# Loading, normalising and turning each x tile in three successive attention passes instead of one

## The chip, the cores and the metric

The kernel runs on one NeuronCore of a Trainium2 chip. The metric is the device time of one execution in microseconds (us), taken as the median of several runs. The engines are named as the profile names them: PE is TensorE (matmuls; PEld its weight loads), DVE is VectorE, ACT is ScalarE, POOL is GpSimd, SP is SyncE, which issues most of the DMAs. All matmuls write to PSUM banks.

## The reference

A batch of 32 sequences of 100 tokens of width 512 passes through a layer norm, a causal cross attention with 16 heads of width 32, and a mixture-of-experts feed-forward. Only the first 100 context rows can be seen through the causal mask. What matters here is the first part:

```python
q = (layernorm(x) @ WQ.T); k = ctx @ WK.T; v = ctx @ WV.T      # 16 heads of 32
scores = einsum(q, k) / sqrt(32), causal; attn = softmax(scores)
y = einsum(attn, v) @ Wfc.T + bfc
x = x + y
# then: layernorm, gate, 16 experts with top-k tokens, a shared expert, and the sum
```

## The kernel before

The 3200 tokens are cut into 8 blocks of 400 tokens (4 sequences), and the 512 columns into 4 chunks of 128 (4 heads). One pass u of the attention loop, u = 0 to 31, stands for block sb = u // 4 and chunk c = u % 4. Everything in the loop is written out by hand under a manual schedule: the order of the program text is the order in which each engine gets its instructions, and every engine works through its own list in order. Matrix products that need full precision are made of three matmuls on a rounded high part and a low remainder of each operand (`mm3`, whose matmul is L55 in the profile); `split` makes the two parts, a cast on ACT (L100) and a subtraction on DVE (L101).

A pass of the loop is a software pipeline over three blocks of work, on PE in this order:

- `scores` of pass u-1 (L236), whose maxima DVE then takes (L247);
- the Q projection of pass u, into a bank of the pool `ps_kv`, copied out by ACT (L226);
- turns of the probabilities of pass u-2 for sequences 0 and 1 (`p_turn`, L277), into banks of the pool `ps_ms`, copied out by ACT (`p_keep`, L282);
- a K projection of a context block needed later, into `ps_kv`, copied out by ACT (L200) and stored;
- turns of the probabilities for sequences 2 and 3;
- a V projection, likewise in `ps_kv` (ACT copy L183). Context blocks have 3 tiles of 128 rows and 4 passes, so in every fourth pass, c = 0, there is no V projection;
- the turn of one x tile (`x_turn`, L167) into a bank of `ps_ms`, which `split` then casts and subtracts (L100, L101) into xnh and xnl, the operands of the Q projection of the next block;
- `values` of pass u-2 (L292), into a bank of `ps_ms`, copied out by ACT at the next pass (`y_keep`, L299).

The pools `ps_kv` and `ps_ms` have two banks each, used in turn; the single `scores` tile takes four.

The softmax of pass u-1 in pass u has two halves. Each is: maxima on DVE (L247), a subtraction on POOL (`sm_sub`, L256), exp on ACT (`sm_exp`, L260), a sum and a reciprocal on DVE (`sm_sum`, L265, L266), and a product on POOL (`sm_mul`, L271).

The x work for a tile of 100 tokens, tile (sb+1, c) in pass u, is: `x_load` one pass earlier (SP, L145, from a pool of five buffers), `x_stats` (DVE L152 and L153, then 1/sigma on POOL, L154 and L155), `x_norm` (DVE L161), and `x_turn`. In the text of the pass x_stats stands between the first two p_keep and the second exp, x_norm ahead of the second sum, x_turn after the V projection. POOL also makes the low parts of the context tiles (`ctx_split`, L135). In pass 13 `load_consts` loads the gate weights gr, which ACT (L568) and DVE (L569) then split. In passes 29 to 31 the first part of the feed-forward is woven in; after that the feed-forward runs, which takes the rest of the time.

Of the kernel before, what the change touches and what calls it, by code (L numbers as in the profile page):

```python
# [7 lines left out]
F32 = mybir.dt.float32  # L8
FR = mybir.dt.float32r
# [6 lines left out]
B, S, D, H, DK = 32, 100, 512, 16, 32  # L16
T = B * S
NE, CAP, FF = 16, 12, 1024
NC4 = D // 128
NFC = FF // 128  # L20
NSB = 8
SB = T // NSB
# [25 lines left out]
def mm3(nc, out, terms, first=True, last=True, by_term=False):  # L48

    seq = [(t, p) for p in ((0, 0), (0, 1), (1, 0)) for t in terms]  # L50
    if by_term:
        seq = [(t, p) for t in terms for p in ((0, 0), (0, 1), (1, 0))]
    n = len(seq)
    for i, (t, (a, b)) in enumerate(seq):
        r = nc.tensor.matmul(out, t[0][a], t[1][b],  # L55
                             start=(first and i == 0), stop=(last and i == n - 1))
    return r.ins


def attention(tc, K, F):  # L60
    nc = tc.nc
    with ExitStack() as ctx, ExitStack() as kvctx:
        def pool(name, bufs, stack=ctx, **kw):
            return stack.enter_context(tc.tile_pool(name=name, bufs=bufs, **kw))
# [19 lines left out]
        xnp = [pool("a_xn0", 1, kvctx, side="right"), xn1]  # L84
        scctx = ctx.enter_context(ExitStack())
        ps_kv = pool("a_kv", BUF["pj"], space=PSUM)
        ps_sc = pool("a_sc", BUF["sc"], scctx, space=PSUM, side="right")
        ps_ms = pool("a_ms", BUF["tr"], space=PSUM)
# [10 lines left out]
        def split(hi, lo, src, eng=None):  # L99
            nc.scalar.copy(hi, src)  # L100
            (eng or nc.vector).tensor_tensor(lo, src, f32(hi), ALU.subtract)  # L101

        def load_w(w, dk):
            r = raw.tile([128, D], F32, name="raw")
            nc.sync.dma_start(r, K.wA[w, :, dk, :])
            return r
# [14 lines left out]
        cur = {}  # L121

        def ctx_load(j, d):
            t0, n = KSTART[j] * 128, KVB[j] * 128
            cr = crp.tile([128, KMAX], F32, name="cr")
            nc.sync.dma_start(cr[:, 0:n], K.ctxT[d, :, t0:t0 + n])
            cur["cr", j, d] = cr
# [9 lines left out]
            cur.setdefault(("cl", j), []).append(l)  # L137

        def x_load(sb, b):
            if b == 0:  # L140
                cur["xh", sb] = xnp[sb % 2].tile([128, NC4, SB], FR, name="xnh")
                cur["xl", sb] = xnp[sb % 2].tile([128, NC4, SB], FR, name="xnl")
            xt = xp.tile([S, D], F32, name="xt")
            r0 = (sb * 4 + b) * S
            nc.sync.dma_start(xt, K.x[r0:r0 + S, :])  # L145
            cur["x", sb, b] = xt

        def x_stats(sb, b):
            st = stp.tile([S, 6], F32, name="bst")
            mv = stp.tile([S, 2], F32, name="mv")  # L150
            rs = stp.tile([S, 1], F32, name="rs")
            nc.vector.bn_stats(st, cur["x", sb, b])  # L152
            nc.vector.bn_aggr(mv, st)  # L153
            nc.gpsimd.tensor_scalar(rs, mv[:, 1:2], EPS, None, ALU.add)  # L154
            nc.gpsimd.tensor_tensor(rs, rs, K.nhalf[0:S, 0:1], ALU.pow)  # L155
            cur["mv", sb, b] = mv, rs

        def x_norm(sb, b):
            xt = cur["x", sb, b]
            mv, rs = cur["mv", sb, b]  # L160
            nc.vector.tensor_scalar(xt, xt, mv[:, 0:1], rs, ALU.subtract, ALU.mult)  # L161

        def x_turn(sb, b):
            xt = cur["x", sb, b]
            tp = ps_ms.tile([128, NC4, 128], F32, name="ms")
            for dk in range(NC4):
                nc.tensor.transpose(tp[:, dk, 0:S], xt[:, dk * 128:(dk + 1) * 128],  # L167
                                    K.ident[0:S, 0:S])
            cs = slice(b * S, (b + 1) * S)
            split(cur["xh", sb][:, :, cs], cur["xl", sb][:, :, cs], tp[:, :, 0:S])  # L170

        def vproj(j, i):
            ps = ps_kv.tile([128, D], F32, name="kv")
            cs = slice(i * 128, (i + 1) * 128)
            ch, cl = cur["ch", j], cur["cl", j]
            mm3(nc, ps, [((ch[d][:, cs], cl[d][:, cs]),
                          (WH[1][:, d, :], WL[1][:, d, :])) for d in range(NC4)],
                by_term=(j == 0))
            return ps

        def vkeep(j, i, ps):
            v = vtp.tile([128, D], F32, name="vt")
            nc.scalar.copy(v, ps)  # L183
            t0 = (KSTART[j] + i) * 128
            nc.sync.dma_start(K.vD[t0:t0 + 128, :], v)
# [17 lines left out]
        def kload(u):  # L203
            sb, c = divmod(u, NC4)
            kt = ktp.tile([128, SB], F32, name="kt")
            nc.sync.dma_start(kt, K.kD[:, c, sb * SB:(sb + 1) * SB])
            cur["k", u] = kt
# [61 lines left out]
        def sm_mul(u, hb):  # L269
            pv, sm = cur["p", u, hb][1], cur["sm", u, hb]  # L270
            nc.gpsimd.tensor_tensor(pv, pv, sm[:, :, None].to_broadcast([S, 8, S]), ALU.mult)  # L271
# [31 lines left out]
        NU = nsb * NC4  # L303
        blocks = range(2, len(KVB))

        def prologue():
            nc.gpsimd.dma_start(mask, K.mask)
            wk = [load_wc(0, 0)]
            for d in range(NC4):
                ctx_load(0, d)  # L310
            wk += [load_wc(0, c) for c in range(1, NC4)]
            wv = [load_w(1, 0), load_w(1, 1)]
            split_wc(0, 0, wk[0])
            for d in range(NC4):
                ctx_split(0, d, nc.vector)
            wv.append(load_w(1, 2))
            for b in range(2):
                x_load(0, b)
            p0 = kproj(0, 0)
            split_wc(0, 1, wk[1])  # L320
            wv.append(load_w(1, 3))
            kkeep(0, 0, p0)
            p0 = kproj(0, 1)
            split_wc(0, 2, wk[2])
            split_wc(0, 3, wk[3])
            for b in range(2, 4):
                x_load(0, b)
            for d in range(NC4):
                ctx_load(1, d)
            wq = [load_wc(2, 0), load_wc(2, 1)]  # L330
            kkeep(0, 1, p0)
            p0 = kproj(0, 2)
            split_w(1, 0, wv[0])
            split_w(1, 1, wv[1])
            kkeep(0, 2, p0)
            p0 = kproj(0, 3)
            split_w(1, 2, wv[2])
            x_stats(0, 0)
            split_w(1, 3, wv[3])
            wq += [load_wc(2, 2), load_wc(2, 3)]  # L340
            kkeep(0, 3, p0)
            p0 = vproj(0, 0)
            x_norm(0, 0)
            x_stats(0, 1)
            x_stats(0, 2)
            x_norm(0, 1)
            x_stats(0, 3)
            for d in range(NC4):
                ctx_split(1, d, nc.vector)
            x_norm(0, 2)  # L350
            x_norm(0, 3)
            vkeep(0, 0, p0)
            p0 = vproj(0, 1)
            split_wc(2, 0, wq[0])
            for d in range(NC4):
                ctx_load(2, d)
            x_load(1, 0)
            vkeep(0, 1, p0)
            for c in range(NC4):
                kkeep(1, c, kproj(1, c))  # L360
                if c == 0:
                    for b in range(4):
                        x_turn(0, b)
                if c:
                    split_wc(2, c, wq[c], nc.gpsimd)
                    ctx_split(2, c - 1)
                else:
                    kload(0)
            ctx_load(3, 0)
            vkeep(1, 0, vproj(1, 0))  # L370

        with tc.manual_schedule():
            prologue()
            for u in range(NU):
                sb, c = divmod(u, NC4)
# [5 lines left out]
                kv = mine and j in blocks  # L381
                vv = kv and ck < KVB[j]
# [2 lines left out]
                jl, dl = divmod(u + NC4 + 2 - KS, NC4)  # L385
                jl += 2
                xs = mine and sb + 1 < nsb
                end = u - (NU - 3)
                if mine:
                    if u > 0:  # L390
                        kload(u)
                    if jl in blocks and (jl, dl) != (3, 0):
                        ctx_load(jl, dl)
                    sn, bn = divmod(u + 5, NC4)
                    if sn < nsb:
                        x_load(sn, bn)
                if FC_AT <= u < FC_AT + NC4:
# [36 lines left out]
                if back is not None:  # L434
# [1 line left out]
                    p_turn(back, 1)  # L436
                    p_keep(back, 0)
                    p_keep(back, 1)
                if xs:
                    x_stats(sb + 1, c)  # L440
                if end == 0:
                    pr.split_y(1)
                if end == 2:
# [16 lines left out]
                if back is not None:  # L460
# [1 line left out]
                    p_turn(back, 3)  # L462
                    p_keep(back, 2)
                    p_keep(back, 3)
                if xs:
                    x_norm(sb + 1, c)
                if a is not None:
                    sm_sum(a, 1)
                    sm_mul(a, 1)
                if end == 0:  # L470
                    pr.split_y(2)
                if end == 1:
# [9 lines left out]
                if vv:  # L482
                    vkeep(j, ck, vproj(j, ck))
                if xs:
                    x_turn(sb + 1, c)
                if end == 0:
                    pr.fc(0)
                if end == 1:
# [563 lines left out]
```

## Time and profile before

| what | us |
|---|---|
| median of 3 runs | 1749.06 (1748.99 to 1749.1) |
| the profiled execution, own time | 1750.64 |
| its span, first to last instruction | 1748.8 |
| attention loop, scores of pass 0 to the last values | about 40 to 394 |
| PE busy over the span | 1698.7 |
| mean granted clock of PE, as a share of full speed | 0.987 |

A row of a timeline gives the start in us, the length, the engine, the line, the operation, what it writes and reads, and in brackets how long the engine was idle before it and what ended that. A run of equal instructions is drawn together (x4). A row of a stretch table gives the stretch, its length, the busy time of PE, PEld, DVE, ACT and POOL, the granted clock, and the DMA share and rate. The chain of waits gives start, length and what was at work.

### The profile page before, as it was taken

The page shows a single profiled execution, that of the slowest core. Times are in us where ns is not written, and L with a number is a line of the kernel's source. Part 1 is how long each engine was busy: PE and PEld are TensorE (multiplying, and loading weights), DVE is VectorE, ACT ScalarE, POOL GpSimd, SP SyncE. Part 2 cuts the span into 40 slices and gives each one's busy share as a digit, 9 for nine tenths or more (in the row PEclk, how much of TensorE's full clock was granted, in tenths as well). Part 3 has the DMA queues.
Part 4 walks back from the last instruction along what each step waited for, and adds up shares of the span by engine and source line. Part 5 has one row for each costly group of instructions (what it writes and reads, how often), then busy time and mean ns, then how long its engine had stood idle before and what let it go on. Part 6 is the DMA issues. An engine that isn't in the chain of part 4 may idle for free.

```text
span 1748.8 us, 27994 instructions
## 1 busy us (share of the span) xinstructions
PE 1698.7 (97%) x11072; PEld 1559.6 (89%) x11072; DVE 885.7 (51%) x2118; ACT 681.2 (39%) x1086; POOL 445.0 (25%) x399
## 2 busy tenths in 40 slices
PE   7999999989999999999999999999999999999996
PEld 6888888878888999999889999999999999999996
DVE  4877777775333333333454444444444444444431
ACT  4555555543112111211234444444444444444431
POOL 3777777661111011101020111110111111011111
PEclk9999999989999999999999999999999999999998
DMA  7444443534111101102154555554555554555531
GB/s 211 136 137 155 131 131 118 164 109 134 70 63 59 55 31 67 61 19 73 46 185 142 163 141 153 158 158 148 148 159 147 163 153 143 156 162 137 137 88 18
DMA packets 82995, 211.13 MB, mean 121 GB/s; under 512 B 9489, under 2 KB 35842, under 8 KB 82864
## 3 DMA queue, kind: packets, MB, share of 16 engines
q1 hardware_dynamic: 71792, 183.87, 32.2%
q0 software_dynamic: 10784, 25.21, 7.9%
q8 instruction: 87, 1.43, 0.3%
q14 instruction: 44, 0.36, 0.1%
q10 hardware_dynamic: 288, 0.27, 0.0%
HBM read 163.71 MB, written 45.60 MB: 120 GB/s over the span
## 4 chain that ended last, share of the span: by engine, by line
PE 91%; DVE 3%; DMA 2%; POOL 2%; ACT 1%; issue 1%; SPq 0%; POOLq 0%; ACTq 0%; DVEq 0%
PE gu L55 46%; PE dn L55 23%; PE kv L55 10%; PE m L55 3%; PE ms L277 2%; PE sc L236 2%; PE ms L292 1%; POOL p L256 1%; DMA big<-yD 1%; PE m L779 1%; DVE p L247 1%; PE ms L167 1%; DVE xt L161 1%; DMA kD<-kk 1%; PE m L894 1%
## 5 line engine op out<-in xcount | busy, mean ns | idle before, releaser
L55 PE MATMUL gu<-xh,whl 128*128 128x384 f32 (+1 forms) x3200 | 645.0, 333 | 1.3 <-ACT g L654 1.3
L55 PEld LDWEIGHTS gu<-xh,whl 128*128 128x128 f32 x3200 | 559.0, 188 | 18.8 <-ACT g L654 1.5
L55 PE MATMUL dn<-whl,hh 128*128 128x512 f32 x1168 | 372.4, 400 | 0.0
L627 DVE TENSOR_TENSOR whl<-wraw,whl 128x1536 fp32r<-128x1536 f32 (+1 forms) x138 | 242.1, 1755 | 241.9 <-ACT whl L626 241.8
L55 PE MATMUL gu<-xl,whl 128*128 128x384 f32 (+1 forms) x1600 | 338.1, 333 | 0.0
L55 PEld LDWEIGHTS gu<-xl,whl 128*128 128x128 f32 x1600 | 280.8, 188 | 0.0
L655 DVE TENSOR_TENSOR g<-g,gu 128x384 f32<-128x384 f32 (+1 forms) x200 | 108.7, 544 | 319.1 <-PE gu L55 316.8
L658 ACT CAST hh<-g 128x384 fp32r<-128x384 f32 (+1 forms) x200 | 100.9, 505 | 431.8 <-DVE g L655 431.8
L55 PEld LDWEIGHTS dn<-whl,hh 128*128 128x128 f32 x1168 | 213.3, 189 | 37.3
L626 ACT CAST whl<-wraw 128x1536 fp32r<-128x1536 f32 (+1 forms) x138 | 201.4, 1460 | 105.3 <-PE dn L55 103.4
L55 PE MATMUL dn<-whl,hl 128*128 128x512 f32 x584 | 230.9, 395 | 0.0
L654 ACT ACTIVATE g<-gu 128x384 f32<-128x384 f32 (+1 forms) x200 | 96.7, 484 | 312.5 <-PE gu L55 312.4
L793 POOL DMA_INDIRECT out_dram<-x,isl x48 | 77.5, 1615 | 365.5 <-ACT x L792 355.8
L659 DVE TENSOR_TENSOR hl<-g,hh 128x384 fp32r<-128x384 f32 (+1 forms) x200 | 111.8, 559 | 114.2 <-ACT hh L658 114.2
L768 POOL DMA_INDIRECT big<-xnD,isl x48 | 48.7, 1015 | 422.5 <-PE m L779 351.8
L55 PEld LDWEIGHTS dn<-whl,hl 128*128 128x128 f32 x584 | 109.8, 188 | 25.9
L271 POOL TENSOR_TENSOR p<-p,sm 100x800 f32<-100x800 f32 x64 | 101.2, 1583 | 51.0 <-DVE sm L266 36.6
L256 POOL TENSOR_TENSOR p<-p,mx 100x800 f32<-100x800 f32 x64 | 96.5, 1528 | 49.7 <-DVE mx L247 49.7
L837 POOL TENSOR_TENSOR x<-x,bfc 128x512 f32<-128x512 f32 x24 | 44.4, 1875 | 248.4 <-DMA x<-x 248.4
L247 DVE CUSTOM_DVE_ANT_0 p<-sc,mask 100x100 f32<-100x100 f32 x512 | 95.6, 257 | 16.6 <-PE sc L236 16.6
L265 DVE TENSOR_REDUCE sm<-p 100x8 f32<-100x800 f32 x64 | 62.7, 980 | 14.1 <-ACT p L260 14.1
L260 ACT ACTIVATE p<-p 100x800 f32<-100x800 f32 x64 | 56.2, 879 | 17.3 <-POOL p L256 17.3
(138 smaller groups left out, 1650.7 us busy)
## 6 DMA issues: line engine op xcount, KB each, us to landing
wraw<-wE SPq DMA_DIRECT2D x136, 768.0 KB, 4.5
xt<-x SPq DMA_DIRECT2D x32, 200.0 KB
vD<-vt SPq DMA_DIRECT2D x25, 256.0 KB, 2.1
kt<-kD SPq DMA_DIRECT2D x32, 200.0 KB, 4.9
v<-vD SPq DMA_DIRECT2D x8, 800.0 KB
x<-x SPq DMA_DIRECT2D x25, 256.0 KB, 5.1
xnD<-xn SPq DMA_DIRECT2D x25, 256.0 KB, 2.0
out_dram<-x SPq DMA_DIRECT2D x25, 256.0 KB, 2.2
```

The lines of the kernel that those rows point to most:

```text
L55: r = nc.tensor.matmul(out, t[0][a], t[1][b], start=(first and i == 0), stop=(last and i == n - 1))
L247: nc.vector.tensor_tensor_reduce(out=p[:, bb, h, :], in0=sc[:, h, cs], in1=mask, scale=ISCALE, scalar=NEG, op0=ALU.add, op1=ALU.max, accum ...
L256: nc.gpsimd.tensor_tensor(pv, pv, mx[:, :, None].to_broadcast([S, 8, S]), ALU.subtract)
L265: nc.vector.tensor_reduce(sm, pv, AX.X, ALU.add)
L271: nc.gpsimd.tensor_tensor(pv, pv, sm[:, :, None].to_broadcast([S, 8, S]), ALU.mult)
L626: nc.scalar.copy(h[:, cs], r[:, cs])
L627: nc.vector.tensor_tensor(l[:, cs], r[:, cs], f32(h[:, cs]), ALU.subtract)
L654: nc.scalar.activation(g[:, 0:t], pg[:, 0:t], AF.Gelu)
L655: nc.vector.tensor_tensor(g[:, 0:t], g[:, 0:t], pu[:, 0:t], ALU.mult)
L658: nc.scalar.copy(hh[:, 0:t], g[:, 0:t])
L659: nc.vector.tensor_tensor(hl[:, 0:t], g[:, 0:t], f32(hh[:, 0:t]), ALU.subtract)
L793: ins = nc.gpsimd.indirect_dma_start(out=self.K.out, out_offset=bass.IndirectOffsetOnAxis(ap=r.isl[:, i:i + 1], axis=0), in_=o, in_offset= ...
```

## The change

The three steps on an x tile are spread over three passes. The tile that pass u turns is now loaded in pass u-2 and normalised in pass u-1. In a pass, `x_stats` and `x_norm` work on the tile of the following pass; x_norm stands after the second sum and product of the softmax instead of ahead of them. The prologue loads two tiles of block 1 instead of one, and does the statistics and the normalisation of the first of them. The pair xnh, xnl is taken from its pool in the first turn of a block, no longer in its first load. In passes without a V projection the turn goes into a bank of `ps_kv`; otherwise it uses `ps_ms` as before. The lines of the functions move by three: x_turn's matmul is L170 in the kernel after, x_norm L158.

```diff
         def x_load(sb, b):
-            if b == 0:
-                cur["xh", sb] = xnp[sb % 2].tile([128, NC4, SB], FR, name="xnh")
-                cur["xl", sb] = xnp[sb % 2].tile([128, NC4, SB], FR, name="xnl")
             xt = xp.tile([S, D], F32, name="xt")
...
-        def x_turn(sb, b):
+        def x_turn(sb, b, own=True):
+            if b == 0:
+                cur["xh", sb] = xnp[sb % 2].tile([128, NC4, SB], FR, name="xnh")
+                cur["xl", sb] = xnp[sb % 2].tile([128, NC4, SB], FR, name="xnl")
             xt = cur["x", sb, b]
-            tp = ps_ms.tile([128, NC4, 128], F32, name="ms")
+            if own:
+                tp = ps_ms.tile([128, NC4, 128], F32, name="ms")
+            else:
+                tp = ps_kv.tile([128, D], F32, name="kv").rearrange("p (c t) -> p c t", c=NC4)
...
+            x_load(1, 1)
             ctx_load(3, 0)
+            x_stats(1, 0)
             vkeep(1, 0, vproj(1, 0))
+            x_norm(1, 0)
...
+                xn = divmod(u + 5, NC4) if u + 5 < NU else None
...
-                    sn, bn = divmod(u + 5, NC4)
+                    sn, bn = divmod(u + 6, NC4)
                     if sn < nsb:
                         x_load(sn, bn)
...
-                if xs:
-                    x_stats(sb + 1, c)
+                if xn:
+                    x_stats(*xn)
...
-                if xs:
-                    x_norm(sb + 1, c)
                 if a is not None:
                     sm_sum(a, 1)
                     sm_mul(a, 1)
+                if xn:
+                    x_norm(*xn)
...
                 if xs:
-                    x_turn(sb + 1, c)
+                    x_turn(sb + 1, c, vv)
```

## The prediction

> **What bounds the kernel now.** I read the page first, then TensorE's (PE's) waits over the attention stage, then the timeline of one pass, then the chain of waits through it. Of the page, section 1 and the clock row of section 2:
>
> ```profile
> PE 1698.7 (97%) x11072; PEld 1559.6 (89%) x11072; DVE 885.7 (51%) x2118; ACT 681.2 (39%) x1086; POOL 445.0 (25%) x399
> ```
>
> PE bounds the whole, so only its idle time and its clock can be won. PE's waits from 100 to 385 us begin with
>
> ```profile
> PE ms L167 <- DVE xt L161: 8.3, 5, 1.7
> ```
>
> that is, five times the turn of an x tile (L167) waits up to 1.7 us for its normalisation on VectorE (L161). Over the span it is 10.4 us in seven waits: 0.45 in pass u=1, and 1.64 to 1.67 in each of u = 4, 8, 12, 16, 20, 24. These six are the passes with c=0, which have no V projection. PE's timeline in u=24 (start, length, instruction, idle time before):
>
> ```profile
> 294.97 0.85 PE L277 MATMUL ms<-ident,p 100*100 100x100 f32 x8
> 297.48 0.53 PE L167 MATMUL ms<-ident,xt 100*128 100x100 f32 x4 [1.67 <-DVE xt L161]
> 298.77 0.96 PE L236 MATMUL sc<-kt,q 32*100 32x100 f32 x32
> ```
>
> The pass began with its scores at 288.98, so it took 9.79 us. Pass u=28 has no V projection and no x work at all, a control inside the kernel:
>
> ```profile
> 337.02 0.85 PE L277 MATMUL ms<-ident,p 100*100 100x100 f32 x8
> 338.51 0.89 PE L292 MATMUL ms<-pt,v 100*32 100x100 f32 x32 [0.64 <-ACT pt L282]
> 339.34 0.96 PE L236 MATMUL sc<-kt,q 32*100 32x100 f32 x32
> ```
>
> From scores at 331.00 it takes 8.34 us: with x gone, the copy of turned probabilities on ScalarE (ACT, L282) ends last. A pass with V takes 10.74, and there the V matmuls (some 2.8 us) hide the x work. The chain of waits in u=24 shows why x is late:
>
> ```profile
> 293.18 1.53 POOL p L256
> ...
> 294.99 0.58 POOL rs L155
> 295.59 1.76 DVE xt L161
> ...
> 297.48 0.53 PE ms L167 x4
> ```
>
> The tile's 1/sigma stands on GpSimd (POOL) behind both subtractions of the softmax, then the normalisation takes 1.76 us. The clock is a second cost. In stretches of 3.4 us (PE's busy time is the third number, the granted clock the third from the end):
>
> ```profile
> 252.00:255.40 3.40, 1.74 (x44) 1.29 (x46) 3.19 (x4) 2.22 (x7) 1.84 (x3) 1.00 0.53 154
> 255.40:258.80 3.40, 3.40 (x39) 3.20 (x40) 2.56 (x26) 0.49 (x1) 2.82 (x3) 0.57 0.43 147
> 122.40:125.80 3.40, 2.29 (x69) 1.96 (x70) 2.63 (x4) 1.85 (x5) 1.84 (x2) 1.00 0.78 220
> ```
>
> The stall of u=20 is followed by 3.4 us at about half clock; that of u=8, shared by two stretches, isn't. After u = 4, 12, 16, 20 the clock falls: starts of slow stretches, 81.5, 167.0, 211.3, 255.4, lie multiples of 3.41 apart. The passes from scores after u=4, 16, 20 take 12.26, 12.01 and 12.23 against 10.74; with 0.24 more for the values matmuls after u=16, about 1.5 us each.
>
> [...] the normalisation takes 0.50 us at the shortest, and 1.75 beside a POOL product.
>
> **The change, part by part.** Order and counts of matmuls are the same; the turn only writes another bank in passes without V. No engine gains or loses an instruction.
>
> (1) Turn in u=4..24. Its tile is now normalised a pass earlier, so the wait on L161 goes. Next late is what u=28 shows: the values wait for the copies. The turn (about 0.44 us of issue) fits into that 0.64. A pass falls from 9.79 to 8.34: 1.45 each. In u = 4, 8, 16, 20, 24: 5 x 1.45 = **7.25 us**. The V-less bank (kv) is free: q was copied out at 292.86, 2.8 before the turn. The kv bank is needed again by the K projection of the next pass, at about 300.6, and the split of the turn should end near 298.2. With kv used, values take the bank of the third probability turn, not the fourth, as in u=28.
>
> (2) u=12 wins nothing. Its successor waits for a load:
>
> ```profile
> 166.73 3.92 DMA gr<-gwT
> ```
>
> ACT sits in front of gr from 166.6 to 170.73, and VectorE (DVE) until 171.0, with softmax behind both. That load is issued after the K copy of u=12, which doesn't move, so the second half of pass 13 still starts at 175.69. PE comes 1.45 us earlier, without the slow stretch, and waits about 2.5 us for a bank that y's copy frees (171.4) and 1.6 before 175.69. This can slow the clock after it: 0 to 1.5, I take **-0.75**.
>
> (3) Clock after u = 4, 16, 20: with 0.2 us of idle time left in those passes, 3 x 1.5 = **4.5 us**. Bounds: 0 (as many slow stretches elsewhere) and 4.5.
>
> (4) DVE's new order: maxima, statistics, sum 0, sum 1, normalise, split of the turn (L101). In u=24 exp 1 on ACT ends at 295.68, so sum 1 runs 295.72 to 296.7, its reciprocal to 296.9[...] The end of the attention shows the same meeting:
>
> ```profile
> 357.01 1.29 POOL L837 TENSOR_TENSOR x<-x,bfc 128x512 f32<-128x512 f32 x1
> 358.26 1.71 POOL L271 TENSOR_TENSOR p<-p,sm 100x800 f32<-100x800 f32 x1
> ```
> ```profile
> 357.65 0.93 DVE L867 TENSOR_SCALAR xn<-x,mv,rs 128x512 f32<-128x512 f32 x1
> ```
>
> DVE waits for the first POOL instruction, goes through at its end (358.58), and the second takes 1.71 instead of 1.52. So here: normalised by about 297.35, product 1 ends 0.25 late at 298.85, the context split on POOL at 299.85, before the next subtraction (300.0). ACT casts the turn at 297.1 to 297.6, L101 ends at 298.2. The next scores start at 297.32, their first maximum can start at 298.35. Nothing late: **0**. If DVE loses, see rival B. In passes with V the turn comes 2.8 us later, which covers both orders.
>
> (5) Start. SP issues one x load (0.32 us) sooner, ahead of a context load used a pass later. It lands perhaps at 40.4 (5.1 us from issue to use at 25.40), so statistics, 1/sigma and normalisation of tile 1 stand ahead of tile 0's split on DVE (41.54 before, about 43 now), with pass 0's maxima behind. POOL's context split, 38.76 before, ends by about 43.4; its reader on PE comes at 44.68. Set against the wait in u=1: from +0.45 to -1.0, I take **0**. Later SP, with five x buffers for three tiles in flight, waits for nothing new.
>
> (6) Taking xnh and xnl at the turn adds no instruction; their last reader, a q projection, is a pass earlier: 0. The last pass's statistics (u=27) fall away against the added ones of the start: 0.
>
> Sum: 7.25 - 0.75 + 4.5 = 11.0 us. The profiled execution took 1750.64 (span 1748.8 and 1.84 around it) and would take 1739.6. The median of the runs, 1749.06, lies 1.58 lower: **1738.1**. All behind the attention is PE-bound or timed from it, and keeps the shift; the long waits at 366 to 384, four slow stretches, may meet other windows: +-1.5.
>
> **Rivals.** A difference of 0.2% is 3.5 us, about what a measurement can tell from no change.
> - A, as summed, 1735.5 to 1740.5: chance 0.70. With slow stretches returning elsewhere, 1742.6: 0.08.
> - B, [...] Normalisation ends near 298.85, L101 at 299.45, and the maxima start 1.1 late. Passes have some 0.1 slack there (copy ends 294.85, next turn 294.97), so the third probability turn of the next pass stalls 1.0. Gain 5 x 0.45 + 4.5 - 0.75 = 6.0: 1743.1. [...] against it, the rows above. 0.13.
> - C, the change doesn't free the turn: L161 was only the last of two close releasers, and something as late takes its place. Gain under 1: about 1748. Pass 28 speaks against. 0.05.
> - D, slower: [...] Normalised at 299.85, L101 to 300.45, maxima 2.1 late, a stall of 2.0 in the next pass: 5 x -0.55 = -2.75, slow clock as before, u=13 -0.75, and perhaps one more slow stretch: about 1754. It decides from 1.55 us of lateness. Against it, again the rows of (4). 0.04.
>
> A and B with their bounds give 1735.5 to 1744.5. Faster 0.90, within 0.2% 0.06, slower 0.04.
>
> **What would show it.** Right: no wait of L170's turn on L158; V-less passes near 8.3 us; normalisation near 0.5 us with product 1 near 1.75; no slow stretches after u = 4, 16, 20; a longer PE idle before 175 in pass 13. Wrong: 1.75 us for the normalisation and waits of probability turns on ACT's copies in passes 5, 9, 17 (B, D); another releaser at the turn (C).

## The result, and the profile after

The kernel after took 1738.3 us (median of 4 runs, 1737.56 to 1739.08), the kernel before 1749.08 beside it: a ratio of 0.9938, 95% interval 0.9926 to 0.9950. The profiled execution after took 1738.44, with a span of 1736.6. Timed again in a later batch (e10, below), the ratio was 0.9937, 0.9923 to 0.9950.

Section 1 of the page after has the same counts of instructions, and PE is busy for 6.4 us less: the stretches at half clock (granted 0.50 or 0.51 in the four that follow the turns of u = 4, 12, 16 and 20 before) are fewer (mean granted clock 0.992, against 0.987 before).

```profile
PE 1692.3 (97%) x11072; PEld 1554.9 (90%) x11072; DVE 858.2 (49%) x2118; ACT 679.3 (39%) x1086; POOL 447.5 (26%) x399
```

PE's waits from 100 to 375 us after; a row names the waiting line, what it waited for, total, times and longest:

```profile
PE ms L280 <- ACT pt L285: 3.7, 3, 2.6
PE ms L892 <- ACT pt L285: 3.5, 2, 3.2
PE ms L280 <- ACT y L302: 2.8, 1, 2.8
PE ms L295 <- ACT pt L285: 2.3, 6, 0.6
```

The turn of x (now L170) waits for its normalisation (now L158) nowhere. The last row is what is next late in V-less passes (c = 0, those without a V projection): the values matmuls stand behind ACT's copies of the turned probabilities. The third row is new, in pass 13. The first two rows lie at the end of the attention, from 335 us on, where the kernel before has such waits too. PE's timeline of u=24 after:

```profile
285.95 0.85 PE L280 MATMUL ms<-ident,p 100*100 100x100 f32 x8
286.64 0.51 PE L170 MATMUL kv<-ident,xt 100*128 100x100 f32 x4
287.47 0.89 PE L295 MATMUL ms<-pt,v 100*32 100x100 f32 x32 [0.33 <-ACT pt L285]
288.30 0.96 PE L239 MATMUL sc<-kt,q 32*100 32x100 f32 x32
```

The turn follows the probability turns without a wait, into a kv bank. From scores at 279.97 to scores at 288.30 the pass takes 8.33 us, the length of the control pass 28. VectorE and GpSimd in the same pass:

```profile
286.69 0.98 DVE L268 TENSOR_REDUCE sm<-p 100x8 f32<-100x800 f32 x1 [0.32 <-ACT p L263]
287.84 0.49 DVE L158 TENSOR_SCALAR xt<-xt,mv,rs 100x512 f32<-100x512 f32 x1
288.65 0.57 DVE L101 TENSOR_TENSOR xnl<-kv,xnh 128x400 fp32r<-128x400 f32 x1 [0.32 <-ACT xnh L100]
```
```profile
286.52 3.19 POOL L274 TENSOR_TENSOR p<-p,sm 100x800 f32<-100x800 f32 x2
289.67 1.01 POOL L135 TENSOR_TENSOR cxl<-cr,cxh 128x384 fp32r<-128x384 f32 x1
```

The normalisation starts 1.32 us after POOL's first product and takes 0.49 us; the two products take 3.19 together instead of some 3.05. It ends at 288.33, 1.38 ahead of the end of the second product: it did not wait for both, as step 4 said.

The lengths of the passes, from scores to scores on PE's timelines, are the instrument for all that follows:

| pass u | before | after | e1 | e2 | e4 | e5 | e6 | e7 | e8 | e9 |
|---|---|---|---|---|---|---|---|---|---|---|
| 1 + 2 | 19.98 | 19.25 | 19.24 | 20.47 | 19.97 | 19.97 | 19.98 | 20.24 | 19.47 | 19.25 |
| 4 | 9.80 | 8.33 | 8.82 | 8.34 | 9.79 | 9.79 | 9.80 | 8.33 | 8.34 | 8.34 |
| 5 | 12.26 | 10.71 | 10.75 | 11.43 | 10.75 | 10.75 | 10.75 | 12.13 | 10.74 | 10.74 |
| 9 | 10.74 | 10.70 | 10.72 | 11.46 | 12.26 | 10.71 | 12.28 | 12.43 | 10.70 | 10.70 |
| 12 | 9.79 | 8.34 | 8.82 | 8.34 | 9.80 | 9.79 | 9.79 | 8.34 | 8.33 | 8.33 |
| 13 | 13.71 | 15.55 | 14.69 | 16.40 | 10.76 | 13.85 | 13.34 | 15.33 | 11.73 | 10.75 |
| 17 | 12.01 | 10.72 | 10.72 | 11.44 | 12.26 | 10.72 | 10.72 | 10.73 | 10.75 | 10.73 |
| 21 | 12.23 | 10.74 | 10.75 | 11.43 | 10.74 | 10.74 | 12.16 | 10.74 | 10.75 | 10.74 |
| 24 | 9.79 | 8.33 | 8.82 | 8.34 | 9.89 | 9.79 | 9.78 | 8.33 | 8.33 | 8.33 |
| 25 | 10.74 | 10.75 | 10.76 | 11.45 | 12.14 | 10.74 | 10.74 | 14.19 | 10.74 | 10.73 |

Passes of before and after that aren't in it are alike, but for u = 8, 16, 20 (as u=24) and the last three. Each column is one profiled execution.

### The profile page after: what moved, and what is told of

The parts are those of the page before. It is cut to its first block, busy times and chain, and to the rows that moved or that the text cites. A ratio compares the mean times of both kernels' runs of the same rounds, so it can differ in the third digit from the quotient of the medians.

```text
span 1736.6 us, 27996 instructions
## 1 busy us (share of the span) xinstructions
PE 1692.3 (97%) x11072; PEld 1554.9 (90%) x11072; DVE 858.2 (49%) x2118; ACT 679.3 (39%) x1086; POOL 447.5 (26%) x399
## 4 chain that ended last, share of the span: by engine, by line
PE 91%; DMA 2%; DVE 2%; ACT 2%; POOL 1%; issue 1%; SPq 0%; POOLq 0%; ACTq 0%; DVEq 0%
PE gu L55 47%; PE dn L55 23%; PE kv L55 9%; PE m L55 3%; PE ms L280 2%; PE sc L239 2%; PE ms L295 1%; PE m L786 1%; DMA big<-yD 1%; POOL p L259 1%; DVE p L250 1%; ACT pt L285 1%; DMA kD<-kk 1%; PE m L901 1%; PE m L892 1%
## 5 line engine op out<-in xcount | busy, mean ns | idle before, releaser
L280 PE MATMUL ms<-ident,p 100*100 100x100 f32 x512 | 56.8, 254 | 6.6 <-ACT pt L285 3.7
```

The lines of the kernel that those rows point to most:

```text
L280: nc.tensor.transpose(tp[0:S, h, 0:S], p[:, b % 2, h, :], K.ident[0:S, 0:S])
```

## The experiments

Theory: the gain is the wait of the turn in V-less passes (1.45 us each, in five of them) and the slow clock that follows some of these waits. Rivals: it is the earlier load, the bank, or VectorE's shorter normalisation in all passes. (The kernel before loads a tile one pass ahead of its turn already, so its three steps stand in two passes, not in one; the change moves the load one pass further and gives the normalisation a pass of its own.)

**e6, the load alone, one pass earlier** (the kernel before with this and the taking of xnh and xnl at the turn):

```diff
-                    sn, bn = divmod(u + 5, NC4)
+                    sn, bn = divmod(u + 6, NC4)
...
+            x_load(1, 1)
             ctx_load(3, 0)
```

> The kernel before, with the loads of x one pass earlier, and nothing else: statistics, normalisation and turn stay together. Theory: the load was never waited for, so no change: 1749.7, V-less passes 9.8. Rival (the transfer is what was late): the gain of the whole change, 1738.

Measured 1749.77 (13 runs) against 1749.51 for the kernel before beside it: ratio 1.0002, 0.9994 to 1.0010. PE's waits from 60 to 330 us still have the old row, under the line numbers of this kernel:

```profile
PE ms L167 <- DVE xt L158: 10.0, 6, 1.7
```

The load alone is worth nothing.

**e7, the rest without it** (the kernel after, loads where they were):

```diff
-            x_load(1, 1)
             ctx_load(3, 0)
...
-                    sn, bn = divmod(u + 6, NC4)
+                    sn, bn = divmod(u + 5, NC4)
```

> The kernel after, with the loads of x where they were before: loaded in the same pass that does the statistics. Theory: a load is issued about 1.5 us into a pass and is in use 5 us later, while the statistics come due 3.9 us after the scores, so VectorE waits some 2.5 us with both sums of the softmax behind; V-less passes stay near 8.3, and the passes after them stall about 1.0 (subtraction on POOL late behind product 1 and the context split): 1742 to 1746. Rival (the load lands in time anyway): 1738.3, V-less passes 8.33 and the next 10.74.

Measured 1752.71 (21 runs), ratio 1.0021, 1.0013 to 1.0028: slower than before, and 7 to 11 us worse than the 1742 to 1746 that I expected. V-less passes are 8.33 us as expected, so the wait at the turn is gone, but the passes after them take up to 14.19, and those ahead of them, 3, 7, 11 and 15, up to 14.44 instead of 10.7. VectorE's waits from 60 to 330 us:

```profile
DVE bst L149 <- DMA xt<-x: 29.3, 16, 5.8
```

I had counted one wait of about 2.5 us in steady passes; the statistics wait up to 5.8, with both sums of the softmax behind them. So the load is worth nothing alone, and without it the rest loses more than it gains. It is also here that rival B's course appears, the normalisation behind both products (VectorE, then POOL, in u=24):

```profile
300.03 2.43 DVE L158 TENSOR_SCALAR xt<-xt,mv,rs 100x512 f32<-100x512 f32 x1
```
```profile
299.16 3.01 POOL L274 TENSOR_TENSOR p<-p,sm 100x800 f32<-100x800 f32 x2 [0.29 <-ACT pt L285]
```

The normalisation starts 0.87 us into the first product and takes 2.43 us instead of 0.50: it ends at 302.46, 0.29 behind the second product. The two products take 3.01 together, undisturbed.

**e1, the turn in an ms bank in all passes:**

```diff
-                    x_turn(sb + 1, c, vv)
+                    x_turn(sb + 1, c)
```

> The kernel after, but the turn of x takes a ms bank in every pass, as before. Theory (the gain is the stall at the turn in V-less passes, and the slow clock behind it): the turn then waits for the copy of the third probability turn and the values for that of the fourth, so V-less passes take about 8.8 us instead of 8.33; 5 x 0.45 = 2.2 us lost, about 1740.5. Rival (banks): what held the turn before was its bank, and the stall returns: 9.8 us a V-less pass, 1745 to 1749.

Measured 1740.89, ratio 0.9946, 0.9932 to 0.9959. The intervals of this kernel and of the kernel after overlap; the lengths of the passes tell them apart. V-less passes take 8.82 us, 0.49 more than in the kernel after. PE in u=24:

```profile
287.06 0.85 PE L280 MATMUL ms<-ident,p 100*100 100x100 f32 x8
288.59 0.56 PE L170 MATMUL ms<-ident,xt 100*128 100x100 f32 x4 [0.68 <-ACT pt L285]
```

The turn now waits for the bank that ACT empties. The bank part of the change is worth 0.49 us a V-less pass, about a third of the 1.46; the rest is the earlier normalisation, with the load that it needs (e7).

**e2, x_norm ahead of the second sum again:**

```diff
+                if xn:
+                    x_norm(*xn)
                 if a is not None:
                     sm_sum(a, 1)
                     sm_mul(a, 1)
-                if xn:
-                    x_norm(*xn)
```

> The kernel after, but x_norm stands ahead of the second sum again; loads, statistics and turns stay spread. Theory: the normalisation again takes 1.75 us behind POOL's product 0, so sum 1, product 1, the context split and the split of the turn all end later, and in passes that follow a V-less one the first subtraction on POOL starts about 1.1 us late and the third probability turn stalls about 1.0; V-less passes stay at 8.3. About 5 us of the gain lost: 1743. Rival (VectorE's time): VectorE's shorter normalisation is the gain itself, in all passes, so that nearly all is lost, 1748. Rival (order is indifferent): 1738.

Measured 1742.42, ratio 0.9958, 0.9944 to 0.9971, as the theory said, though the single stall was 0.7 us (11.43 to 11.46 in passes after a V-less one, instead of some 10.74) where I had put 1.0; pass 2 lost 1.2 as well. The normalisation is at 1.75 us again:

```profile
290.65 1.75 DVE L158 TENSOR_SCALAR xt<-xt,mv,rs 100x512 f32<-100x512 f32 x1 [0.20 <-POOL rs L152]
```

V-less passes stay at 8.33 or 8.34, and passes that don't follow one stay at their old length. So VectorE's 1.25 us saved per pass is no gain in itself; in this kernel it counts only where the next pass begins early.

**e5, PE busy during the wait** (the kernel before; the result of the added matmuls is not used):

```diff
+                if xs and not vv and u > 0:
+                    idle = ps_kv.tile([128, D], F32, name="kv")
+                    for i in range(6):
+                        nc.tensor.matmul(idle[:, 0:SB], WH[2][:, i % NC4, 0:128],
+                                         cur["xh", sb][:, i % NC4, :], start=True, stop=True)
                 if xs:
                     x_turn(sb + 1, c)
```

> The kernel before, with six matmuls of 400 columns whose result is not used, in a kv bank ahead of the turn in V-less passes (about 1.0 us inside the 1.65 us of waiting). Theory: V-less passes stay at 9.8 us, but the clock no longer falls after u = 4, 16, 20; these passes take 10.74 instead of 12.0 to 12.3. 4.5 us gained: 1744.6. Rival (the slow stretches have another cause): no gain, 1749, or slower by up to 6 x 0.1 if the fill delays the turn.

Measured 1746.29 (21 runs), ratio 0.9979, 0.9972 to 0.9986: 3.4 us gained with every V-less pass still at 9.79 and nothing else done. PE after the wait in u=20:

```profile
253.36 0.53 PE L167 MATMUL ms<-ident,xt 100*128 100x100 f32 x4 [0.54 <-DVE xt L161]
253.82 0.89 PE L292 MATMUL ms<-pt,v 100*32 100x100 f32 x32
254.65 0.96 PE L236 MATMUL sc<-kt,q 32*100 32x100 f32 x32
255.54 0.99 PE L55 MATMUL kv<-xnh,wh 128*128 128x400 f32 x4
```

The scores take 0.96 us and the first Q matmuls 0.99; before they took 1.17 and 1.70:

```profile
256.36 1.70 PE L55 MATMUL kv<-xnh,wh 128*128 128x400 f32 x4
```

With 0.54 us of idle time left, no V-less pass is followed by a slow one: the granted clock is 1.00 in all stretches of 3.4 us from 27.2 to 363.8. That separates the two parts of the gain: the slow clock came with the stall of 1.65 us, not with the 0.54 left of it, and is worth 3.4 us on average (2.4 to 4.9 by the interval). Which stalls are followed by it changes from one execution to the next: u = 4, 12, 16, 20 in the kernel before, 8 and 20 in e6, 8, 16 and 24 in e4.

Where the stall lies tells which. In each profile the slow stretches start on a grid of 3.41 us: in the kernel before at 81.8, 167.1, 211.5 and 255.9, which are 85.3, 44.4 and 44.4 us apart, 25, 13 and 13 times 3.41 to 3.42. Of the 18 stalls in these three profiles, nine leave PE idle for at least 1.5 us within one stretch of that grid, and the next stretch is slow in all nine. The other nine are shared by two stretches, with at most 1.44 us of idle time in one, and none is followed. This is no limit for all waits: in e5, 1.74 us of idle time in the stretch from 341.7 is followed by full clock.

**e3, gr loaded early** (the kernel after):

```diff
+                if u == FC_AT + 1:          # pass 10
+                    nc.sync.dma_start(F.gr, K.gwT)
```

and its load in pass 13 taken out. (gr are the gate weights, gw their two parts.)

> The kernel after, with the load of gr (131 KB in 64-column rows) issued in pass 10 instead of pass 13; its split stays in pass 13. Theory: pass 13 (15.55 us) waits for this load alone and falls to 10.8, so 4.7 us less: about 1733.6. Rival (the softmax chain of pass 13 is late anyway): under 1 us gained, 1737.5.

(128 x 64 fp32 values are 33 KB; the size given there is wrong.) Measured 1735.94, ratio 0.9920, 0.9907 to 0.9934: half of what I expected. Pass 13 fell from 15.55 to 12.91. The chain of waits through it:

```profile
160.77 1.64 POOL p L274
162.42 1.43 POOL cxl L135
163.84 0.26 POOL gw L575
164.10 0.02 issue
164.13 0.25 ACT gw L576
```

With the load out of the way, the clearing of gw on POOL is next, behind a product and a context split, and ACT and VectorE wait for it as they did for the load.

**e8, gw off the path of the softmax** (the kernel after):

```diff
+                if u == FC_AT + 1:
+                    F.gw_load()        # load of gr, clearing of gw
...
+                if u == FC_AT + NC4:
+                    F.gw_split()       # at the end of the pass, behind ctx_split
```

with the load, the clearing and the split of gw taken out of `load_consts`.

> The kernel after, with gr loaded and gw cleared in pass 10, and gw split at the end of pass 13. In the run with the early load alone pass 13 still took 12.91 us: gw was cleared on POOL behind product 1 and the context split, ahead of y's copy and the maxima. Theory: with this gone as well pass 13 takes 10.75, so 4.8 us less than the kernel after: about 1733.5. Rival: something else in pass 13 is late, 12.9 stays, 1735.9.

Measured 1734.15, ratio 0.9909, 0.9895 to 0.9924. Pass 13 took 11.73: a further 1.2 gone, 1.0 left. VectorE at the end of pass 12:

```profile
161.31 1.48 DVE L591 TENSOR_TENSOR wfl<-raw,wfh 128x512 fp32r<-128x512 f32 x1 [0.45 <-ACT wfh L590]
162.71 0.56 DVE L101 TENSOR_TENSOR xnl<-kv,xnh 128x400 fp32r<-128x400 f32 x1
```

This split of weights begins during POOL's second product, which ends at 162.24, and takes 1.48 us; in the kernel before, where it begins 0.23 us ahead of that product, it takes 0.65. The maxima of pass 13 begin behind it; e9 tries whether this is what is left.

**e4, the same edit in the kernel before.**

> The kernel before, with gr loaded and gw cleared in pass 10, and gw split at the end of pass 13. Theory: the stall of u=12 (9.79) stays, pass 13 falls from 13.71 to 10.74, or to some 12.2 where a slow stretch follows the stall, so 1.5 to 3.0 us are gained: about 1746.9 against 1749.7 for the runs of before beside it. Against e8 it shows whether the stall of u=12 and the load cover each other: if not, both gain the same.

Measured 1746.78 (21 runs), ratio 0.9986, 0.9980 to 0.9993: 2.7 us gained, where the kernel after gains over 4 from it (1738.3 to 1734.15). In profiles, passes 12 and 13 together fall from 23.50 to 20.56 here, by 2.94, and from 23.89 to 20.06 there, by 3.83. The two gains overlap within their intervals, so it is the passes that show it: without the load of gr in pass 13 the change takes 1.48 us from passes 12 and 13 (20.56 in e4, 19.08 in e9 below), with it nothing (23.50 before, 23.89 after). So the two waits covered each other: the change freed 1.45 us in pass 12 and handed it to the wait for gr.

**e9, e8 with one more move:** the passes that split the output projection's weights are 9, 10, 11 and 13 instead of 9 to 12, and gw is split in pass 14. **e10** is the kernel after once more.

> The kernel of e8, with the split of the fourth part of the output projection's weights moved from pass 12, which has no V projection, to pass 13, and gw's split to pass 14. In e8 pass 13 still took 11.73 us: in pass 12 VectorE's split of these weights (1.48 us[...]) stood ahead of the split of the turn and the next maxima. Theory: pass 13 takes 10.75, 1.0 us less than e8: about 1733.2. Rival: the split makes the pass after it late wherever it stands: 1734.2.

> The kernel after, unchanged, timed beside the same runs of before as e9. Theory: 11 to 12 us less than before; V-less passes 8.33 again, whatever the slow stretches of the start and the end of the attention do.

e9: 1733.59 (4 runs), ratio 0.9908, 0.9893 to 0.9923; pass 13 takes 10.75. The 0.98 us less in that pass is seen in the profile; between the medians of e8 and e9 it is 0.6, within their intervals. e9 beats both kernels. e10: 1738.93 (5 runs) against 1749.27, 10.3 us less where I had expected 11 to 12; V-less passes 8.33 or 8.34, pass 13 15.31.

## Why the prediction was right

The forecast was 1738.1, the median 1738.3. The mechanism was right: the wait of the turn is gone from V-less passes, and with it the slow clock behind u = 4, 16 and 20. That the sum agrees to 0.2 us is luck, for several of its terms were off by 0.4 to 2.4 us, with both signs. By its steps:

- (1) 1.45 us in each of five V-less passes: 9.80, 9.79, 10.03, 9.80, 9.79 became 8.33 or 8.34, so 1.46 each, and 0.24 more in u=16, where values ran slowly before. (This 0.24 is counted under step 3.) The control pass had named the next late thing, the copies, and it is the one that is there.
- (2) Nothing from u=12: passes 12 and 13 went from 23.50 to 23.89, a loss of 0.39 where I put 0.75. PE waits 2.76 us for y's bank, where I had 2.5:

```profile
168.33 0.90 PE L280 MATMUL ms<-ident,p 100*100 100x100 f32 x4 [2.76 <-ACT y L302]
168.93 1.63 PE L55 MATMUL kv<-cxh,wh 128*128 128x384 f32 x4
```

  The slow stretch came, but fell on a K projection (1.63 us instead of 0.94), and the further wait of 1.6 us that I had put behind it isn't there.
- (3) The clock: passes 5, 17 and 21 lost 1.55, 1.29 and 1.49 us, with the 0.24 of u=16 4.57 in all, against 4.5. This fit was to one execution. Over many runs e5 gives 3.4 (2.4 to 4.9), so for the median the term was probably sized about 1 us too high, within the bounds given. The slow stretches themselves begin at 81.8, 167.1, 211.5 and 255.9 in the trace, up to 0.5 us later than the starts that I gave; their spacing holds.
- (4) VectorE's order costs nothing. I had put the normalisation of u=24 at 296.85, inside POOL's first product (295.53 to 297.05) with the second to follow, and estimated from one such meeting that it would end 0.3 us behind the first. This was right in the kernel after, where all 24 normalisations from 60 to 330 us took 0.79 us at most, and the second product took 1.65 us in most, where I had 1.75. It is no rule: in e7 the normalisation waited for both products in 11 of 25 cases. Rival B was a possible course. In the kernel after the normalisation starts late in the first product (1.3 us in most), in those 11 cases of e7 earlier (0.58 to 0.87).
- (5) The start: I took 0 with a range from +0.45 to -1.0; passes 1 and 2 together gained 0.73, outside that. The load wasn't waited for (statistics began at 40.74, straight behind a normalisation, 5.3 us after the issue at 35.41), and the split of the turn ended 0.5 us later against the scores, not some 1.5.
- What has no step: pass 1 starts 1.73 us later in the profile after than before (42.50 against 40.77). The shift is there by 26.0 us, ahead of all that the change moves: in the profile after a slow stretch from 21.4 us (granted clock 0.50 to 24.8) lies on matmuls that run at full clock before (1.00). e10 starts at 41.43. The last three passes lost 0.64 (counted in the passes' sum below), and the rest of the kernel gained 2.36, with its slow stretches in other places: more than the +-1.5 that I had set for it, and together with the start it nearly cancels. 11.57 in the passes - 1.73 + 2.36 is the 12.2 us between the spans.

C fell with the waits after: nothing as late took the place of L161 at the turn. D, where the normalisation waits for the context split as well, did not occur in the kernel after, though in e7 the normalisation waits for both products.

## What to carry to other kernels

Look for a pass of the same loop that lacks the suspected work: its length is what the others fall to, and its last wait is what comes next. A stall on PE can cost about as much again through the clock (here 1.46 us, and 1.29 to 1.55 in the pass after it for u = 4, 16 and 20), so price the two apart; filling the stall with idle matmuls measures the second alone (3.4 us for all passes in e5). A wait that stands behind another on a different engine takes the gain back, as the load of gr did in pass 13, and removing it afterwards can yield more than it would have before. When work is moved a stage earlier, check whether its load must move with it: here the load was worth nothing alone (e6), and without it the change lost (e7).

## What the runs showed of the hardware that I had not expected

A normalisation on VectorE that starts during the first of two POOL products does not always end soon after that one. In the kernel after, it starts about 1.3 us into the first product in most cases and takes 0.50 us. In e7 it starts 0.86 or 0.87 us into it in ten cases, and 0.58 in one, and ends 0.3 us behind both products, after 2.42 to 2.72 us; in the cases of 0.92 us and more it takes 0.50 to 0.88. Yet in the kernel before a normalisation that started 0.64 us into an addition of 1.29 took 0.93 and ended 1.39 ahead of the end of the product behind the addition, and in the kernel after all four splits of weights (L581), which started 0.72 us into a product of 1.65, took 1.48 and ended 0.86 to 0.88 ahead of the end of the context split that comes next on POOL. Whether it is how early the second instruction stands ready on POOL was not tried, and stays open.

After a stall of 1.64 to 1.67 us PE's granted clock can be 0.50 or 0.51 for 3.41 us (the kernel before, after u = 4, 12, 16 and 20), and after one of 0.54 it wasn't in any of six passes (e5). The same stall was followed by it in nine of 18 cases, those where at least 1.5 us of it lay in one stretch of the grid of 3.41 us.
